# When the layers start beside the sorts, and which rows are asked for ahead of one scatter: two orders changed in a graph kernel

## The chip, the cores and the metric

One core of a Trainium2 chip runs the whole program in one launch. The metric is the device time of that launch in microseconds (us). The engines are named as the profile names them: PE (matrix products), DVE (vector work), ACT (activations and copies), POOL (here: indirect DMAs and one small memset) and SP (plain DMAs). Each engine works through its own queue in order; an instruction that waits holds everything behind it on that engine.

## What is computed

There are 16 graphs of 1024 nodes with 64 channels, an adjacency matrix each, and two residual layers.

```
h = relu(layernorm(x))
# layer 0
adj_d = adjacency with self loops, thinned by a rule on ranks and degrees
s     = values of the live neighbours, sorted per node and channel
agg   = 0.25*quantile(s, 0.25) + 0.5*quantile(s, 0.5) + 0.25*quantile(s, 0.75)
x     = x + mask * (relu((h + agg) @ W1 + b1) @ W2 + b2)        # 64 -> 128 -> 64
# layer 1
h  = relu(layernorm(x))
x1 = bn(relu(adj @ (h  @ W1) + b1))
x2 = bn(relu(adj @ (x1 @ W2) + b2))
x3 = bn(relu(adj @ (x2 @ W3) + b3))
x  = x + relu(concat(x1, x2, x3) @ Wl + bl)
```

## The kernel before

The 16 graphs are treated as 8 pairs. A loop over the pairs thins the adjacency, orders the nodes by degree, and computes the quantiles by sorting networks on DVE (`quantiles`, line L1186 is its compare). The nodes of a pair fall into groups by degree:

- Blocks whose neighbours' rows PE gathers by matrix products (`sort_block`; `sort_pairs` for the few nodes of highest degree, which two or four pairs share; the last of these, the *tails* of pairs 4 to 7, are the 16 nodes of highest degree in each graph).
- Groups of nodes whose neighbours' rows POOL fetches by indirect DMA (`fetch_nodes`, `sort_nodes`). A group has 17, 19 or 21 slots. For each slot POOL issues two *asks* (L1486), numbered a=0 and a=1, and then a memset of a tiny row (L1498), which only keeps the pace. The ask a=0 of a slot waits for the compare that DVE's program had reached when the slot was asked for; the ask a=1 has no such wait and is ordered only behind the memset of the slot before.

The results of a group are written to a buffer in memory, `agg_d`, by indirect scatters on POOL (L1368). The tails' eight scatters (two for each pair, tile `o_tails`) come from `store_tails`.

Behind the loop over pairs stands the last part. There the sorts of pair 7 and the shared groups are still to be done, and beside them runs the generator `later`, which does all of layer 1 and the MLP of layer 0 for pair after pair:

- `load(p)` issues loads on SP (L1693 `xt`, L1694 `h`, L1695 `agg`, L1702 `mk`). The load of `agg` waits for all scatters of that pair.
- `first(p)` is `first_layer`: L1594 adds `h` to `agg`, L1583 transposes, L1603 and L1607 are the MLP's products, L1608, L1610 and L1611 finish layer 0, L624 to L632 are the layernorm, and L1583 transposes its result (`pt`).
- `second(p)` loads the adjacency (`adjT`, L1715) and runs `next_layer`: for each of three layers L1636 `pw` and its three parts (L1637, L1640, L1641, L1642), then 96 products `pg` (L1652) in two halves with L1656 and L1657 behind each; then `pf` (L1668), L1672, L1675 and the output (L1677). Each `pw`, each half of `pg`, and the end is a step of its own.

`weave(sort, (steps, count, first, end), ...)` writes the order by hand: while the parts of one sort are issued, it takes `count` steps of another generator, spread over the given stretch of the sort. `steps(n)` takes `LATE_SHARES[n]` steps of `later`, and `asking(group, first, end, share)` takes a share of a group's slots. What is left at the end of the sorts is run by `ahead.rest()`. Nothing of this is an instruction's final place: a scheduler places the issued instructions on each engine by their order and the stated dependences, and scatters are issued under high priority.

The last part handles the groups in this order: the tails (`steps(5)`), `then[0]` (group 1 of pair 6, 19 slots, `steps(6)`), the shared block of pair 7 (`steps(7)`), `then[1]` (the group that pairs 6 and 7 share, 21 slots, `steps(8)`), `then[2]` (pair 7, 17 slots, `steps(9)`) and `then[3]` (pair 7, 19 slots, `steps(10)`). So the asks of `then[1]` are 42, of `then[2]` 34, of `then[3]` 38.

The lines that put the tails' scatters ahead of later asks are these:

```
                    if sent_ahead[0] is not None:
                        follow(asked, sent_ahead[0])
                        sent_ahead[0] = None
```

`sent_ahead` is set behind the tails' `send`, and the first ask that is issued after it follows the last of these scatters.

Of the kernel before, what the change touches and what calls it, by code (L numbers as in the profile page):

```python
# [56 lines left out]
TAILS = {4: (0, 4), 7: (4, 8)}  # L57
TAIL = (1008, 1024, 21, 42)

MID = len(BLOCKS) - 1  # L60
# [349 lines left out]
def graph_layers_kernel(ctx: ExitStack, tc: tile.TileContext, ins, out: bass.AP):  # L410
    nc = tc.nc
    x_d, adj_d, mask_d = ins["x"], ins["adj"], ins["nodemask"]
    NB, N, _ = x_d.shape
# [3 lines left out]
    NP = NB // 2  # L417
# [62 lines left out]
    for i in range(2 * len(NODES) - 1):  # L480
        _, _, least, slots = NODES[i % 2 if i < 4 else 2]
# [136 lines left out]
    def rows_of(ap):  # L618
        return ap.rearrange("(t p) c -> p t c", p=P)
# [837 lines left out]
    def sort_pairs(n, first, end, g, pools):  # L1457

        work, ps, rows = pools
        block = (BLOCKS + (TAIL,))[n]  # L1460
        W = block[1] - block[0]
        whole = (end - first) * W
        t = rows.tile([P, plan(block)[3], whole], F32, tag="t", bufs=1, name="t_pairs")
        agg = work.tile([P, whole], F32, tag="agg_pairs", name="agg_pairs")
        z = part_z[n] if n == MID else part_z[n][:, :, first:end]
        yield from quantiles(work, block, (g, t), z.rearrange("p q p2 w -> p q (p2 w)"), agg)
        if n > MID:
            store_tails(first, end, agg, pools)
            return
        for p in range(first, end):  # L1470
            waiting.append((p, agg, slice((p - first) * W, (p - first + 1) * W), block[0]))
# [54 lines left out]
    def asking(fetched, first, end, share=1.0):  # L1526

        return fetched[4], math.ceil(share * NODES[fetched[1]][3]), first, end

    def sort_nodes(fetched, pools):  # L1530

        work, ps, rows = pools
        pairs, i, g, z, ask = fetched
        ask.rest()
        j0, j1, _, slots = block = NODES[i]
        W = g.shape[2]
        t = rows.tile([P, plan(block)[3], W], F32, tag="t", bufs=1, name="t_nodes")
        agg = work.tile([P, W], F32, tag="agg_nodes", bufs=1, name="agg_nodes")
        yield from quantiles(work, block, (g, t), z, agg, W // C)
        waiting_nodes.append((pairs, i, agg))  # L1540
# [17 lines left out]
    def weave(sort, *others):  # L1558


        share, taken = 0.0, [0] * len(others)

        def due(share):
            for i, (steps, count, first, end) in enumerate(others):
                while taken[i] < count and first + (end - first) * taken[i] / count <= share:
                    steps.step()
                    taken[i] += 1

        due(0.0)
        for part in sort:  # L1570
            share += part
            due(share)
        due(1.0)
# [106 lines left out]
    def later(pools, keep, done):  # L1680

        one, ps = pools


        def load(p):
            assert p < done.sent
            xt = one.tile([P, NT, 2, C], F32, tag="xt", bufs=2, name="xt")
            h = one.tile([P, NT, 2, C], F32, tag="h", name="h_late")
            agg = one.tile([P, NT, 2, C], F32, tag="agg", name="agg")
            mk = one.tile([P, NT, 2], U8, tag="mk", name="mk")  # L1690
            for x in range(2):
                b = 2 * p + x
                nc.sync.dma_start(out=xt[:, :, x, :], in_=rows_of(x_d[b]))  # L1693
                nc.sync.dma_start(out=h[:, :, x, :], in_=rows_of(h_d[b][:, :]))  # L1694
                load = nc.sync.dma_start(out=agg[:, :, x, :], in_=rows_of(agg_d[p][x * N : (x + 1) * N, :]))  # L1695
                for sent in agg_sent[p]:
                    tc.add_manual_dep(
                        load.ins, sent.ins.name,
                        mybir.DependencyInfo(mybir.DependencyClass.Sync, mybir.DependencyReason.DATA),
                        reason="aggregates of all nodes",  # L1700
                    )
                nc.sync.dma_start(out=mk[:, :, x], in_=mask_d[b])  # L1702
            return xt, h, agg, mk

        def first(xt, h, agg, mk):
            mask = one.tile([P, NT, 2], F32, tag="mask", name="mask")
            nc.vector.tensor_copy(mask, mk)
            cur = yield from first_layer(pools, xt, h, agg, mask)
            return xt, cur

        def second(p, x2, cur):
            adjT = []
            for x in range(2):
                adjT.append(one.tile([P, NT, N], F8, tag=f"adjT{x}", name=f"adjT{x}"))
                nc.sync.dma_start(out=adjT[x], in_=adjT_d[2 * p + x][:, :, :])  # L1715
            yield
            yield from next_layer(pools, [out[2 * p], out[2 * p + 1]], adjT, x2, cur)

        loaded = load(0)
        yield  # L1720
        given = yield from first(*loaded)
        for p in range(NP):
            now = Steps(second(p, *given))
            now.step()
            yield
            ahead = None
            if p + 1 < NP:
                loaded = load(p + 1)
                for _ in range(5):
                    now.step()  # L1730
                    yield
                ahead = Steps(first(*loaded))
            while now.step():
                yield
                if ahead is not None and ahead.step():
                    yield
            if ahead is not None:
                ahead.rest()
                given = ahead.result
# [146 lines left out]
    with ExitStack() as stack:  # L1886
        keep = stack.enter_context(tc.tile_pool(name="keep", bufs=1))
        pools = (
            stack.enter_context(tc.tile_pool(name="work", bufs=1)),
            stack.enter_context(tc.tile_pool(name="ps", bufs=1, space=PSUM)),  # L1890
            stack.enter_context(tc.tile_pool(name="rows", bufs=1)),
        )
        with ExitStack() as inner:
# [19 lines left out]
            for p in range(NP - 1):  # L1913
# [3 lines left out]
                def steps(n):  # L1917
                    return ahead, SHARES[n], 0.0, 1.0
# [6 lines left out]
                both = rows_of_pairs(MID, p, p + 1, p, pools, "g1")  # L1925
# [4 lines left out]
                if p in TAILS:  # L1930
                    tails = rows_of_pairs(MID + 1, *TAILS[p], TAILS[p][1], pools, "g0")
# [13 lines left out]
        with ExitStack() as inner:  # L1945
            one = inner.enter_context(tc.tile_pool(name="late", bufs=1))
            late = (one, inner.enter_context(tc.tile_pool(name="ps_late", bufs=2, space=PSUM)))
            done = Pair()
            done.sent = 4
            ahead = Steps(later(late, keep, done))  # L1950
            def steps(n):
                return ahead, LATE_SHARES[n], 0.0, 1.0

            st = sts[-1]
            weave(sort_block(st, 0, pools), gather_block(st, 1, pools), asking(nodes, 0.0, 0.9), steps(0))
            weave(sort_nodes(nodes, pools), gather_block(st, 2, pools), steps(1))
            nodes = fetch_next()
            then = [fetch_next("r0")]
            weave(sort_block(st, 1, pools), asking(nodes, 0.0, 0.9), steps(2))
            send_nodes()  # L1960
            both = rows_of_pairs(MID, NP - 1, NP, NP - 1, pools, "g1")
            weave(
                sort_block(st, 2, pools), gather_block(st, MID, pools, into=both), asking(then[0], 0.0, 0.9), steps(3)
            )
            tails = rows_of_pairs(MID + 1, *TAILS[NP - 1], NP - 1, pools, "g0")
            weave(sort_nodes(nodes, pools), gather_block(st, MID + 1, pools, into=tails[:, :, -TW:]), steps(4))
            then += [fetch_next(), fetch_next("s"), fetch_next("s")]
            weave(
                sort_pairs(MID + 1, *TAILS[NP - 1], tails, pools), asking(then[1], 0.0, 0.9), steps(5),
            )  # L1970
            send(pools)
            sent_ahead[0] = last_sent[0]
            done.sent = NP - 2
            weave(sort_nodes(then[0], pools), asking(then[2], 0.1, 1.0, 0.6), steps(6))
            send_nodes()
            weave(sort_pairs(MID, NP - 1, NP, both, pools), asking(then[2], 0.0, 0.8), asking(then[3], 0.8, 1.0, 0.1), steps(7))
            send(pools)
            weave(sort_nodes(then[1], pools), asking(then[3], 0.0, 1.0, 0.5), steps(8))
            send_nodes()
            done.sent = NP - 1  # L1980
            weave(sort_nodes(then[2], pools), asking(then[3], 0.0, 0.9), steps(9))
            send_nodes()
            weave(sort_nodes(then[3], pools), steps(10))
            send(pools)
            done.sent = NP
            ahead.rest()
# [49 lines left out]
```

## Time and profile before

| what | value |
|---|---|
| median of 7 runs | 2841.92 us (2833.01 to 2853.05) |
| the profiled execution | 2821.8 us, its span 2819.9 us |
| granted PE clock over the span | 0.864 |
| DVE busy | 2347.3 us (83%) |
| PE busy | 2161.1 us (77%) |
| POOL busy | 1712.0 us (61%) |
| ACT busy | 1618.8 us (57%) |

Times inside the execution are counted from the span's start. The profiled execution is 20 us shorter than the median of the runs. Of the span, the last part with `later` takes the stretch from about 2160 us to the end; the sorts end at 2712.75 us, and 107.15 us follow in which only `later` runs. "Idle before" in a row is how long the engine stood still just before the instruction, with what ended that.

### The profile page before, as it was taken

Reading aid. Unit: us, or ns where it says so; the run is one execution under the profiler, and the core shown is the slowest. Engines: PE = TensorE matmul, PEld = TensorE weight load, DVE = VectorE, ACT = ScalarE, POOL = GpSimd, SP = SyncE. Lnnn points to the kernel's source line nnn. Section 1 sums busy time; section 2 is a strip of 40 time slices with the busy share of each in tenths; the row PEclk is TensorE's granted clock in tenths of the full one; section 3 lists DMA queues with packets and bytes.
Section 4 is the critical chain, followed back from the end, with each engine's and each line's share of the span. In section 5 each row is a group of like instructions: output and inputs, shape, how many; then the busy total and the mean of one; then the engine's idle time right before and its main releaser. Section 6 shows DMA issues by size and latency. Waiting matters only on the chain. (4 is left out here: it accounts for less than half of the span.)

```text
span 2819.9 us, 54826 instructions
## 1 busy us (share of the span) xinstructions
PE 2161.1 (77%) x21220; PEld 1382.0 (49%) x21220; DVE 2347.3 (83%) x5452; ACT 1618.8 (57%) x3255; POOL 1712.0 (61%) x1570
## 2 busy tenths in 40 slices
PE   4668977796789679868974588579858899738888
PEld 3435554454455446535642455355526565425555
DVE  6358998788889889998979999889986988939863
ACT  4564877476758667785867367767673324213222
POOL 7225766485928663774576748674865387988200
PEclk9869988897799789969986799789869988879899
DMA  5114222222322132224252133142213136213221
GB/s 158 57 42 134 59 74 70 86 72 62 76 83 88 48 90 74 83 68 119 63 79 57 28 93 89 47 112 75 74 41 72 24 78 93 67 24 77 68 61 47
DMA packets 262766, 205.43 MB, mean 73 GB/s; under 512 B 218721, under 2 KB 219105, under 8 KB 258401
## 3 DMA queue, kind: packets, MB, share of 16 engines
q1 hardware_dynamic: 178528, 133.61, 16.3%
q0 software_dynamic: 40960, 62.37, 9.2%
q10 hardware_dynamic: 43008, 5.87, 1.8%
q8 instruction: 168, 2.75, 0.4%
q14 instruction: 102, 0.83, 0.1%
HBM read 148.89 MB, written 52.81 MB: 72 GB/s over the span
## 5 line engine op out<-in xcount | busy, mean ns | idle before, releaser
L1486 POOL DMA_INDIRECT g_nodes<-rows_d,rows_listed x744 | 978.3, 1315 | 716.4 <-DVE prod L1198 267.0
L1270 PE MATMUL pg<-s,hp 128*64 128x496 fp8e4 (+5 forms) x8064 | 756.3, 339 | 149.0 <-ACT hp L764 53.0
L1270 PEld LDWEIGHTS <-hp 128*64 128x64 bf16 x8064 | 458.1, 114 | 390.7 <-ACT hp L764 73.9
L1498 POOL MEMSET rest_row<- 1x768 bf16 x372 | 289.2, 777 | 0.1
L1652 PE MATMUL pg<-adjT,xw 128*64 128x512 fp8e4 x2304 | 280.4, 392 | 5.9 <-ACT xw L1641 2.9
L1245 DVE TENSOR_SCALAR s<-r 128x3200 uint16<-128x3200 uint16 (+2 forms) x192 | 206.7, 1085 | 65.1 <-PE pg L1270 48.1
L983 POOL DMA_INDIRECT live_d<-edge,place x128 | 151.7, 1185 | 113.7 <-issue 55.7
L1274 ACT ACTIVATE g<-pg 128x400 f32<-128x400 f32 (+3 forms) x168 | 83.9, 499 | 223.2 <-PE pg L1270 154.2
L1652 PEld LDWEIGHTS <-xw 128*64 128x64 bf16 x2304 | 133.2, 113 | 137.2 <-issue 25.8
L850 ACT ACTIVATE edge<-a 128x1024 fp8e4<-128x1024 uint32 x128 | 135.3, 1058 | 97.6 <-DMA a<-in_adj 95.1
L942 ACT ACTIVATE edge<-q,bias 128x1024 fp8e4<-128x1024 f32 x128 | 142.0, 1110 | 56.9 <-PE q L937 51.0
L1186 DVE TENSOR_TENSOR t<-g 128x800 f32<-128x800 f32 (+9 forms) x184 | 168.3, 928 | 2.8 <-ACT g L1274 0.8
L915 ACT ACTIVATE stays<-cs,back 128x1024 f16<-128x1024 f32 x128 | 138.4, 1113 | 48.9 <-PE cs L911 35.5
L1341 PE MATMUL pg<-s,hp 128*64 128x384 bf16 (+14 forms) x1872 | 152.6, 303 | 16.5 <-DVE s L1310 11.5
L1186 DVE TENSOR_TENSOR t_nodes<-g_nodes 128x256 f32<-128x256 f32 (+6 forms) x192 | 125.4, 663 | 47.7 <-DMA g_nodes<-rows_d,rows_listed 33.7
L1018 PE MATMUL pt<-ident_h,lp 128*128 128x128 bf16 x1024 | 106.8, 274 | 72.6 <-ACT liveT L1024 32.9
L1186 DVE TENSOR_TENSOR g<-t 128x992 f32<-128x992 f32 (+7 forms) x176 | 160.2, 935 | 2.3
L969 ACT ACTIVATE stays<-keys,minus 128x1024 fp8e4<-128x1024 f32 x120 | 134.2, 1119 | 45.8 <-PE keys L954 32.5
L1368 POOL DMA_INDIRECT agg_d<-o,node_of x96 | 136.2, 1418 | 33.8 <-issue 24.9
L857 PE MATMUL ptE<-ident_h,one 128*128 128x128 bf16 x1024 | 84.2, 233 | 77.0 <-DVE one L854 60.9
L1656 ACT ACTIVATE xT<-pg,c_L_gnn_b 128x512 f32<-128x512 f32 x48 | 32.9, 685 | 186.8 <-PE pg L1652 163.1
L1310 DVE TENSOR_SCALAR s<-r 128x192 bf16<-128x192 bf16 (+11 forms) x544 | 115.2, 307 | 29.4 <-remote 15.2
(272 smaller groups left out, 5218.5 us busy)
## 6 DMA issues: line engine op xcount, KB each, us to landing
a<-in_adj SPq DMA_DIRECT2D x128, 512.0 KB
lp<-live_d POOLq DMA_DIRECT2D x32, 514.0 KB
adjT_d<-edgeT SPq DMA_DIRECT2D x16, 1024.0 KB
adjT<-adjT_d SPq DMA_DIRECT2D x16, 1024.0 KB
g_nodes<-rows_d,rows_listed POOLq DMA_INDIRECT x744
room<-in_x SPq DMA_DIRECT2D x16, 256.0 KB
h_again<-h_d SPq DMA_DIRECT2D x16, 256.0 KB
xt<-in_x SPq DMA_DIRECT2D x16, 256.0 KB
```

What stands on the lines that cost most here:

```text
L850: nc.scalar.activation(edge[:, t, :N], a[:, :].bitcast(U32), AF.Sign, accum_out=found[:, 0, b, t : t + 1], saturate=False)
L915: nc.scalar.activation(stays[:, t, :], cs, AF.Abs, bias=back[:, t : t + 1], scale=2.0)
L942: nc.scalar.activation(edge[:, t, :N], q, AF.Relu, bias=bias(-2.0), accum_out=nv[:, t : t + 1], saturate=False)
L983: sent = nc.gpsimd.indirect_dma_start(out=live_d[b][:, :], out_offset=bass.IndirectOffsetOnAxis(ap=place[:, t : t + 1], axis=0), in_=edge[ ...
L1186: sorted_by[0] = nc.vector.tensor_tensor(view(bufs, o, n1, n2), view(bufs, a, n1, n2), view(bufs, b, n1, n2), ALU.max if op else ALU.min)
L1245: nc.vector.tensor_scalar(s[:, j, :, us, :], st.r[0][:, :, us, j0:j1], abs(k - 3), 0x0808, ALU.logical_shift_right if k > 3 else ALU.logic ...
L1270: summed = nc.tensor.matmul(out=pg[x * C : (x + 1) * C, those, :], lhsT=st.hp[:, part, x, u, :], rhs=picked, start=(i == 0 and part == 0), ...
L1341: summed = nc.tensor.matmul(out=pg[x * C : (x + 1) * C, ks, w0:], lhsT=st.hp[:, part, x, u, :], rhs=s[:, ks, x, u, w0:], start=(whole and ...
L1368: sent = nc.gpsimd.indirect_dma_start(out=agg_d[p][:, :], out_offset=bass.IndirectOffsetOnAxis(ap=rows, axis=0), in_=data, in_offset=None)
L1486: asked = nc.gpsimd.indirect_dma_start(out=g[:, k, a * C : (a + 1) * C], out_offset=None, in_=rows_d[st.p][:, :], in_offset=bass.IndirectO ...
L1498: rested[0] = nc.gpsimd.memset(rest_row, 0.0)
L1652: nc.tensor.matmul(out=pg[cs, :], lhsT=part[:, u, cs], rhs=adjT[x][:, u, sl], start=(u == 0 and k == 0), stop=(u == NT - 1 and k == len(xw ...
```

## The change

Two things are changed in the order that is written by hand; no arithmetic, tile or buffer changes.

In `later`, `first(p+1)` starts after two further steps of `second(p)` and not after five. So it alternates with the second half of the first layer's products, the second layer's `pw` and the second layer's products, where it alternated before with the second half of layer 2 and with layer 3.

In the last part, rows are asked for later: of `then[1]` a share of 0.3 beside the tails' sort, and the rest beside the sort of `then[0]`; of `then[2]` and `then[3]` correspondingly later.

```diff
@@ later
                 loaded = load(p + 1)
-                for _ in range(5):
+                for _ in range(2):
                     now.step()
                     yield
                 ahead = Steps(first(*loaded))
@@ last part
             weave(
-                sort_pairs(MID + 1, *TAILS[NP - 1], tails, pools), asking(then[1], 0.0, 0.9), steps(5),
+                sort_pairs(MID + 1, *TAILS[NP - 1], tails, pools), asking(then[1], 0.0, 0.9, 0.3), steps(5),
             )
             send(pools)
             sent_ahead[0] = last_sent[0]
             done.sent = NP - 2
-            weave(sort_nodes(then[0], pools), asking(then[2], 0.1, 1.0, 0.6), steps(6))
+            weave(sort_nodes(then[0], pools), asking(then[1], 0.1, 1.0), steps(6))
             send_nodes()
-            weave(sort_pairs(MID, NP - 1, NP, both, pools), asking(then[2], 0.0, 0.8), asking(then[3], 0.8, 1.0, 0.1), steps(7))
+            weave(sort_pairs(MID, NP - 1, NP, both, pools), asking(then[2], 0.0, 1.0, 0.6), steps(7))
             send(pools)
-            weave(sort_nodes(then[1], pools), asking(then[3], 0.0, 1.0, 0.5), steps(8))
+            weave(sort_nodes(then[1], pools), asking(then[2], 0.0, 0.5), asking(then[3], 0.5, 1.0, 0.3), steps(8))
             send_nodes()
             done.sent = NP - 1
             weave(sort_nodes(then[2], pools), asking(then[3], 0.0, 0.9), steps(9))
```

## Prediction

> **What bounds the kernel now.** I read the page's 40 slices first, to see where DVE, the busiest engine, is not full near the code that changes.
>
> ```profile
> PE   4668977796789679868974588579858899738888
> DVE  6358998788889889998979999889986988939863
> POOL 7225766485928663774576748674865387988200
> ```
>
> A slice is 70.5 us. The 36th (2467 to 2538 us) is the dip: DVE and PE at 3, POOL at 8. The last two slices are the tail, in which PE is full and DVE is not. Next, the stretches around the dip (busy us of PE, PEld, DVE, ACT, POOL):
>
> ```profile
> 2467.00:2490.00 23.00, 7.04 (x56) 3.69 (x52) 4.43 (x11) 1.96 (x3) 18.83 (x22) 0.72 0.10 19
> 2490.00:2510.00 20.00, 0.00 (x0) 0.00 (x0) 0.00 (x0) 0.00 (x0) 16.44 (x20) 0.50 0.13 19
> 2608.00:2679.00 71.00, 59.81 (x426) 37.99 (x425) 62.65 (x125) 19.90 (x42) 20.40 (x17) 0.88 0.29 68
> 2679.00:2713.00 34.00, 23.32 (x171) 16.76 (x171) 33.18 (x68) 6.97 (x11) 0.00 (x0) 0.85 0.32 96
> 2713.00:2765.00 52.00, 51.45 (x416) 31.04 (x410) 22.66 (x31) 15.00 (x25) 1.91 (x2) 1.00 0.20 60
> ```
>
> For 20 us only POOL works. Later POOL has room (20.40 of 71, then nothing), DVE bounds up to 2713, PE behind it. The timeline names the stalled instruction, and the chain that ended last says what it waits for:
>
> ```profile
> 2472.11 0.41 DVE L1186 TENSOR_TENSOR t_nodes<-t_nodes 128x256 f32<-128x256 f32 x1
> 2513.70 1.23 DVE L1594 TENSOR_TENSOR agg<-agg,h_late 128x1024 f32<-128x1024 f32 x1 [41.18 <-issue]
> ```
>
> ```profile
> 2507.28 1.81 DMA agg_d<-o_tails,node_of
> 2509.33 2.96 DMA agg<-agg_d
> 2512.29 1.42 issue
> ```
>
> L1594 is the first instruction of pair 4's `first`. It stands in DVE's queue ahead of most of `then[0]`'s sort, waits for the `agg` load, and that waits for pair 4's two tails' scatters. POOL's timeline shows why those are late: `o_tails` was written by 2461.87 (ACT's row), but POOL was at asks.
>
> ```profile
> 2502.37 0.94 POOL L1486 DMA_INDIRECT g_nodes<-rows_d,rows_listed  x1 [0.30 <-issue]
> 2503.61 0.94 POOL L1486 DMA_INDIRECT g_nodes<-rows_d,rows_listed  x1 [0.30 <-issue]
> 2504.86 0.94 POOL L1486 DMA_INDIRECT g_nodes<-rows_d,rows_listed  x1 [0.30 <-issue]
> 2506.11 0.87 POOL L1368 DMA_INDIRECT agg_d<-o_tails,node_of  x1 [0.30 <-issue]
> 2507.28 0.86 POOL L1368 DMA_INDIRECT agg_d<-o_tails,node_of  x1 [0.30 <-issue]
> ```
>
> **Step 1: POOL ahead of the tails' scatters.** From 2383.32 to 2506.11 POOL issued, without a long pause, 60 asks, 38 memsets and 2 other scatters. In the built order of the changed kernel the same start is followed by 45 asks, 38 memsets and 2 scatters. Only a=0 asks move behind the tails (14 of `then[1]`, one of `then[2]`): an a=1 ask is ordered only behind the memset before it, so all 21 of `then[1]` and all 17 of `then[2]` stay in front. An ask takes 0.94 + 0.30 = 1.24 us where DVE is idle; over the whole stretch it is (122.8 - 38 x 0.89 - 2 x 1.4)/60 = 1.44, with a memset at 0.73 + 0.16 and a scatter at the page's mean of 1.4. So 15 fewer are worth 18.6 to 21.6 us. I take 18.6, as what falls away is the end of the queue, where DVE is idle. First scatter: 2506.1 - 18.6 = 2487.5.
>
> **Step 2: the order among the scatters.** Before, pair 4's are the 1st and 2nd of eight; in the built order they are the 1st and 6th. The sixth starts 5.8 us behind the first (the eight start 1.15 us apart). From pair 4's last scatter to L1594 is 2513.70 - 2507.28 = 6.4 us. So L1594 starts at 2487.5 + 5.8 + 6.4 = 2499.7, 14.0 us sooner; 41 us of stall become some 24, since the layers and sort that are issued ahead of L1594 also grow by six DVE instructions (2.7 us).
>
> **Step 3: DVE from L1594 to the last sort's end.** Before, this takes from 2513.70 to 2712.75, 199.0 us. I add up for its 404 instructions the distance from start to start that the same shape has when it runs back to back (0.34 us for 256 columns, 0.60 for 512, 1.14 for 1024): 182.1 us, so 17 us are idle (4.2 of it at one xT, 2.7 at one L1608). The changed order has 394 instructions here, 176.8 us: six run ahead of L1594 (2.7 us, inside the stall), and four now stand behind the sort's end (two L1672 and L1675 of pair 5 and a small one, 2.6 us). The idle time I can't derive: `first` now lies beside layer 2 and not layer 3, so every wait in it moves. Bounds: 5 us if the better spread hides most, 17 as before, more by the rivals below. I take 14, near the row of before. The last sort ends at 2499.7 + 176.8 + 14 = 2690.5, 22.2 us sooner.
>
> POOL must keep up with that. Behind `then[0]`'s sort it has about 35 asks, 19 memsets and 4 scatters to issue before the last row of `then[2]`: 35 x 1.24 + 19 x 0.89 + 4 x 1.17 = 65 us, or 73 with 1.44 an ask. DVE needs 78 us of back-to-back work (the same sums) from there to the first compare of `then[2]`. So the asks fit, with 5 to 13 us to spare; I cost them at nothing. If that cover goes, the shortfall is added to the sort's end.
>
> The Trainium skill (GPSIMD Engine Reference, Key points) says that POOL shares its SBUF interfaces with DVE and contends with DVE instructions that have two SBUF inputs, as every compare has. The trace agrees (1.24 us an ask with DVE idle, 1.44 on average), and the rule speaks against this change: 15 asks leave the time when DVE is idle for the time of its compares. By the rule they cost 15 x 0.2 = 3 us more of POOL, by the fit above still nothing.
>
> **Step 4: the tail.** Before, 107.15 us follow the last sort. Two things lengthen it.
>
> ```profile
> 2706.88 1.97 PE L1583 MATMUL pt<-ident,agg 128*128 128x128 f32 x8 [10.68 <-DVE agg L632]
> 2708.67 3.16 PE L1636 MATMUL pw<-wl,chan 128*128 128x128 f32 x16
> 2711.77 10.79 PE L1652 MATMUL pg<-adjT,xw 128*64 128x512 fp8e4 x96
> ```
>
> Before, pair 6's first layer starts at 2711.77, 1 us ahead of the sort's end. In the built order its `pw` needs a PSUM buffer that pair 5's L1672 frees, and this L1672 now stands behind the sort's last instruction: two L1672 (1.2), `pw`'s second half and its three parts follow (1.0 + about 1.7), so `pg` starts 3.9 us behind the sort's end: 4.9 us later relative to it. Then pair 7's `first` lies in layer 2 of pair 6. PE's work is the same, but the layernorm's last transposes (`pt`) now head PE's queue in front of layer 3 while DVE finishes L1608 to L632 (10.3 us from py's end to L632's); the half of layer 2 that is still queued covers most, and 2 to 4 us stay open. The rest (`pf`, pair 7's own 52.8 us) is unchanged. Together 7 to 9, I take 8: 115.2 us.
>
> **The sum.** 2690.5 + 115.2 = 2805.7 against 2819.9: -14.2 us. In the pairs 0 to 3 of `later` (2160 to 2472 us) only `range(2)` acts, and there POOL's asks set the pace (a wait of 60 us in POOL's queue ends at 2226, and then POOL is busy to 2365); back-to-back work to L1594 is 274.4 us against 272.0, the six instructions of step 2: cost nothing. The profiled execution becomes 2807.6; it was 0.7% below the median, so the same difference makes 2841.9 - 14.2 = 2828 of the median.
>
> **Rivals.**
> *The asks come back as a wait on rows* (no change, 0.18). Behind the tails POOL's row at 2515.94 shows an ask of 1.91 us plus 0.30 while DVE sorts. If all 35 took 2.2: 77 + 17 + 5 = 99 us against 78 plus some 5 of idle, so `then[2]` waits 16 us, and the sum is about +2. For it: that row. Against it: the mean of 1.44.
> *PE's queue* (slower, 0.28). The transposes that wait for L632 stand in front of layer 3's products for pairs 5, 6 and 7, not in front of the next pair's.
>
> ```profile
> PE pt L1583 <- DVE agg L632: 36.3, 6, 12.3
> ```
>
> Today these waits are 6 us each, 12.3 at most. If each of three pairs pays 6 more, on PE and so on DVE's next xT, the 14.2 are gone by +4; at the full 12.3 it is 23 slower. It decides from 22.7/3 = 7.6 us a pair. Against it: DVE has its sort to do meanwhile, except for pair 7, where I have charged it.
> *The idle time of step 3 shrinks to 5* (0.09): -23 us, 2819.
>
> **How the numbers follow.** About 0.3% (8.5 us) is what a measurement of this kernel can tell from no change. The forecast has 0.45, its own range 2815 to 2832 (idle 5 to 17, 1.24 to 1.44, tail 7 to 9). Faster: 0.43 of it, 0.09, and 0.02 of the rows' case, 0.54. Same: 0.02, 0.10 of the rows' case, 0.05 of PE's queue, 0.17. Slower: 0.06 and 0.23, 0.29. The range reaches from 2814 to 2852: it leaves out the worst of PE's queue above and a gain beyond 28 below.
>
> **What would show it.** Right: the idle before pair 4's L1594 falls from 41.2 to about 24; its scatters are the 1st and 6th; POOL is busy through 2550 to 2620; the last sort ends near 2690 and 115 us follow, with `pg` of pair 6 behind the sort's end. Wrong: a wait of DVE's sort for `g_nodes` of `then[2]` or `then[3]`; PE waiting over 8 us for L632 in pairs 5 or 6; a tail over 120 us; or L1594 later than 2505.

## The result and the profile after

The changed kernel takes 2847.24 us (median of 26 runs) against 2840.09 us of the kernel before: ratio 1.0034, with a 95% interval of 1.0017 to 1.0051. It is slower by about 10 us where 14 us less were forecast. On another chip the same pair gave 1.0008 (0.9986 to 1.0029). The time lies inside the forecast range; the sign is wrong.

The profiled execution is 2847.6 us with a span of 2845.8 us. First its slices:

```profile
PE   4668977796788579769964697589768996748888
DVE  6368998798889889898979998888977996949962
POOL 7334856486828664773677748666774597958400
```

The dip of DVE in the 36th slice (2490 to 2561 us) is still there, 4 where 3 stood, and the 34th (2348 to 2419 us) has fallen from 8 to 6: idle time was spread, not removed. The timeline of DVE names two large waits where there was one:

```profile
2386.74 0.58 DVE L1657 TENSOR_SCALAR xT<-xT,bn_s,c_L_gnn_be 128x512 f32<-128x512 f32 x1 [23.73 <-issue]
2518.26 1.23 DVE L1594 TENSOR_TENSOR agg<-agg,h_late 128x1024 f32<-128x1024 f32 x1 [24.13 <-issue]
```

The row of L1594 is the stall that the change was priced on: 41.18 us before, 24.13 now, and some 24 were forecast. The row of L1657 is new. ACT's timeline shows where it comes from:

```profile
2354.82 1.07 ACT L1586 COPY chan<-pt 128x512 f32<-128x512 f32 x2 [0.25 <-issue]
2385.85 0.27 ACT L1389 COPY o<-pt_agg 128x128 f32<-128x128 f32 x1 [29.96 <-DMA agg_d<-o,node_of]
2386.01 1.27 ACT L1656 ACTIVATE xT<-pg,c_L_gnn_b 128x512 f32<-128x512 f32 x2
```

L1389 copies a block's aggregates into the tile `o`, of which there are three; this copy waits for the scatter of the copy three before it, and that scatter is in POOL's queue behind asks. L1656 stands behind it on ACT, and L1657 on DVE waits for L1656. Before, ACT reached the same copy later, when the scatter was done.

POOL at the tails' scatters, and PE at the start of pair 6 (the same places before are shown in the prediction):

```profile
2506.09 0.87 POOL L1368 DMA_INDIRECT agg_d<-o_tails,node_of  x1 [0.30 <-issue]
```

```profile
2710.81 1.97 PE L1583 MATMUL pt<-ident,agg 128*128 128x128 f32 x8 [11.45 <-DVE agg L632]
2730.37 2.11 PE L1636 MATMUL pw<-wl,chan 128*128 128x128 f32 x16
2732.41 3.35 PE L1652 MATMUL pg<-adjT,xw 128*64 128x512 fp8e4 x26
```

The first tails' scatter is at 2506.09, as late as before, although POOL needs less time for what is ahead of it: 107.3 us from the first ask of `then[1]`, against 122.8. That ask starts 16 us later, and 7 of these were behind already in the loop over the pairs. To leave them out, times are counted below from a common start where it is named: the last L1207 of the shared block that is sorted ahead of the last part. On this count the ask starts at 276.1 us, 9 us later than before (267.2). The new wait on ACT is not the cause: without it the ask starts no sooner (279.4 with a fourth buffer for `o`, 278.8 in a second execution of the order of before), so the profiled execution of before was early here. The last sort ends at 2728.2, and pair 6's first `pg` starts 4.2 us behind it.

Three rows of the chain that ended last matter for the reading of both profiles. Before:

```profile
2603.36 8.92 another core or an unknown queue
```

After:

```profile
2523.41 11.34 another core or an unknown queue
2651.95 8.74 another core or an unknown queue
```

In each of them ACT stands still for some 9 to 11 us, and the trace names nothing that holds it. Such a halt is put down to "remote" in the list of waits, here of ACT, first before and then after:

```profile
ACT g_pairs L1346 <- remote: 29.0, 7, 7.9
```

```profile
ACT g_pairs L1346 <- remote: 36.2, 6, 12.6
```

They do not belong to an order of the kernel. Of the sixteen traces of this case four have 31 to 41 such waits each, in which ACT alone stands for 81 to 116 us; the other twelve have none. The four are before, after and the two runs on the place and the tail apart, taken where the kernel before takes 2840 and 2853 us in the median; beside the twelve it takes 2767 to 2786 us.

The table sets the stretches of the forecast beside each other, for these two executions and for a second one of each order without such halts (of before: the run with a fourth buffer, in which DVE, ACT and POOL have the same instructions in the same order; the second ones are from two chips).

| stretch, us | before | before, again | forecast | after | after, again |
|---|---|---|---|---|---|
| first ask of `then[1]` to first tails' scatter | 122.8 | 124.9 | 104.2 | 107.3 | 108.4 |
| idle before pair 4's L1594 | 41.2 | 53.6 | 24 | 24.1 | 23.5 |
| L1594 to the last sort's end | 199.0 | 190.8 | 190.8 | 209.9 | 193.3 |
| last sort's end to the end | 107.2 | 106.9 | 115.2 | 117.6 | 115.5 |

### The profile page after: what moved, and what is told of

Its sections match the earlier page's. It is cut to its first block, busy times and chain, and to the rows that moved or that the text cites. A ratio compares the mean times of both kernels' runs of the same rounds, so it can differ in the third digit from the quotient of the medians.

```text
span 2845.8 us, 54808 instructions
## 1 busy us (share of the span) xinstructions
PE 2155.7 (76%) x21220; PEld 1380.9 (49%) x21220; DVE 2344.3 (82%) x5452; ACT 1619.9 (57%) x3255; POOL 1744.3 (61%) x1570
## 4 chain that ended last, share of the span: by engine, by line
DVE 32%; PE 22%; ACT 8%; issue 4%; DMA 3%; another core or an unknown queue 2%; POOL 1%; SPq 0%; DVEq 0%; ACTq 0%; POOLq 0%
PE pg L1270 6%; PE pg L1652 5%; DVE t L1186 4%; DVE t_nodes L1186 4%; DVE g_nodes L1186 3%; DVE g L1186 3%; DVE s L1245 3%; DVE g_pairs L1186 2%; DVE t_pairs L1186 2%; ACT stays L969 2%; DVE s L1310 2%; ACT liveT L1024 1%; PE pg L1341 1%; PE py L1607 1%
## 5 line engine op out<-in xcount | busy, mean ns | idle before, releaser
L1486 POOL DMA_INDIRECT g_nodes<-rows_d,rows_listed x744 | 1007.2, 1354 | 726.7 <-DVE prod L1198 271.7
L983 POOL DMA_INDIRECT live_d<-edge,place x128 | 164.7, 1287 | 99.5 <-issue 50.6
L1652 PEld LDWEIGHTS <-xw 128*64 128x64 bf16 x2304 | 139.0, 114 | 131.3 <-issue 24.4
L1186 DVE TENSOR_TENSOR t_nodes<-g_nodes 128x256 f32<-128x256 f32 (+6 forms) x192 | 125.3, 664 | 53.6 <-DMA g_nodes<-rows_d,rows_listed 52.7
L1368 POOL DMA_INDIRECT agg_d<-o,node_of x96 | 127.4, 1327 | 30.0 <-issue 25.0
L1656 ACT ACTIVATE xT<-pg,c_L_gnn_b 128x512 f32<-128x512 f32 x48 | 32.9, 687 | 193.8 <-PE pg L1652 183.7
L1018 PEld LDWEIGHTS <-lp 128*128 128x128 fp8e4 x1024 | 91.3, 125 | 100.5 <-issue 86.5
```

Of the source, the lines that this page charges most:

```text
L983: sent = nc.gpsimd.indirect_dma_start(out=live_d[b][:, :], out_offset=bass.IndirectOffsetOnAxis(ap=place[:, t : t + 1], axis=0), in_=edge[ ...
L1018: nc.tensor.matmul(out=pt[:, u, :], lhsT=lp[:, u * P : (u + 1) * P], rhs=ident_h, start=True, stop=True)
L1186: sorted_by[0] = nc.vector.tensor_tensor(view(bufs, o, n1, n2), view(bufs, a, n1, n2), view(bufs, b, n1, n2), ALU.max if op else ALU.min)
L1486: asked = nc.gpsimd.indirect_dma_start(out=g[:, k, a * C : (a + 1) * C], out_offset=None, in_=rows_d[st.p][:, :], in_offset=bass.IndirectO ...
L1652: nc.tensor.matmul(out=pg[cs, :], lhsT=part[:, u, cs], rhs=adjT[x][:, u, sl], start=(u == 0 and k == 0), stop=(u == NT - 1 and k == len(xw ...
```

## The experiments

All ratios are to the kernel before, run beside them on the same chip; the runs were made on several chips, so that only ratios and stretches are compared from one chip to another.

**The wait for a fourth buffer.** Two kernels differ from after and before in this:

```diff
-        o = work.tile([P, P], F32, tag="o", bufs=3, name="o")
+        o = work.tile([P, P], F32, tag="o", bufs=4, name="o")
-    rest_row = const.tile([1, 768], BF16, name="rest_row")
+    rest_row = const.tile([1, 768], U8, name="rest_row")
```

(the same for `o_tails`; the second edit makes room for the buffer, and the memset then writes a whole 0). For the changed kernel:

> The changed kernel with a fourth buffer for the tile o (the paced memset row made one byte an element to find the room; no other edit, instructions in the same order). Theory A (ACT's copy into o waits for a scatter behind POOL's asks, and that holds xT, DVE and PE): the idle of 23.7 us before L1657 at 2387 goes, the tails' sort ends 10 to 20 us sooner than in the changed kernel, and the time is 8 to 18 us below the changed kernel, so 0 to 8 us below the kernel before. Theory B (POOL's asks are the pace in that stretch, the copy only happens to stand there): the wait moves to another instruction, the time is within 3 us of the changed kernel. Theory C (PE's queue and the tail decide): the stretch to the tails' sort gets shorter but the end gains under 3 us.

For the kernel before:

> Control: the kernel before with the same fourth buffer for o and the same memset row. All theories: no wait at o is there to take away, so within 3 us of the kernel before. If the one byte memset alone changes POOL's pace, it shows here.

Measured: the changed kernel with the buffer 0.9980 (0.9958 to 1.0003), the kernel before with it 0.9992 (0.9974 to 1.0010). The row on DVE in the changed kernel with the buffer:

```profile
2454.79 1.23 DVE L1594 TENSOR_TENSOR agg<-agg,h_late 128x1024 f32<-128x1024 f32 x1 [43.09 <-DMA agg<-agg_d]
```

The wait at L1657 is gone, and DVE reaches the end of the tails' sort 29 us sooner than in the second execution of the changed kernel (333.5 against 363.0 us from the common start). But L1594 starts only 10 us sooner (390.4 against 400.2), as its stall grows from 23.5 to 43.1: POOL sets it. POOL's first ask of `then[1]` starts at the same time in both (279.4 and 279.7); what is shorter is the stretch from there to the tails' scatters (98.7 against 108.4 us), in which more asks run while DVE stands still. So theory A was right on the place. Its price isn't settled by this run: 0.9980 is 8 to 15 us below the changed kernel's 1.0008 and 1.0034, which A forecast, but these ratios are from other chips and their intervals are nearly as wide. The control shows that neither the buffer nor the memset of one byte an element changes the kernel before.

**The two halves of the change.**

```diff
 asks alone:    for _ in range(5), and the new asking(...) lines
 layers alone:  for _ in range(2), and the old asking(...) lines
```

> The asks of the change with the layers as before (five steps). Theory A: the copies into o stand where they stood before, no wait there; pair 4's L1594 starts 14 us sooner and the tail is as before, so 10 to 18 us below the kernel before. Theory B: asks pushed behind come back as waits, within 4 us of before. Theory C: as A, since the tail is unchanged, 10 to 18 us below.

> The layers of the change (two steps) with the asks as before. Theory A: the wait at the copy into o is there (20 to 25 us idle before an L1657 near 2387), the stall at pair 4's L1594 stays at about 40 us, the tail is 8 to 11 us longer: 15 to 25 us above the kernel before. Theory B: only the tail, 5 to 10 us above. Theory C: 8 to 11 us above.

Measured: the asks alone 0.9931 (0.9904 to 0.9958), the layers alone 1.0072 (1.0043 to 1.0101). The stall with the asks alone, and the two waits with the layers alone:

```profile
2476.68 1.23 DVE L1594 TENSOR_TENSOR agg<-agg,h_late 128x1024 f32<-128x1024 f32 x1 [19.90 <-issue]
```

```profile
2324.44 0.59 DVE L1657 TENSOR_SCALAR xT<-xT,bn_s,c_L_gnn_be 128x512 f32<-128x512 f32 x1 [24.84 <-ACT xT L1656]
2473.74 1.23 DVE L1594 TENSOR_TENSOR agg<-agg,h_late 128x1024 f32<-128x1024 f32 x1 [43.66 <-DMA agg<-agg_d]
```

This splits the change into a gain of some 19 us and a loss of some 20. What was called one change is two of opposite sign. With the asks alone L1594 stands 22 instructions further back in DVE's queue than in the change, and 28 further than before: 22 compares of the sort and 6 instructions of the layers more run ahead of the stall, and from L1594 to the last sort's end it takes 176.9 us.

**The layers alone with the fourth buffer** (the two edits above together).

> The layers at two steps with the asks as before and the fourth buffer for o. Theory A (the copy into o holds ACT): the idle of 24.8 us before an L1657 goes. With the stall at pair 4's L1594 set by POOL, that stall takes up what is saved there (43 to 60 us instead of 43.7), so of the 18 us over the kernel before some 5 to 15 are saved. Rival (POOL alone sets the time of L1594 whatever ACT does): under 3 us are saved.

Measured: 1.0068 (1.0048 to 1.0088), about as without the buffer. The row:

```profile
2468.05 1.22 DVE L1594 TENSOR_TENSOR agg<-agg,h_late 128x1024 f32<-128x1024 f32 x1 [62.36 <-DMA agg<-agg_d]
```

Most of what ACT's wait gave back, the stall took: 43.7 became 62.4, and L1594 starts 7 us sooner from the common start (409.2 against 415.9), which the ratios do not show. This speaks for the rival of theory A, POOL; the intervals leave room for the lower end of what A forecast.

**Pair 7's first at five steps**, the fourth buffer kept:

```diff
-                for _ in range(2):
+                for _ in range(5 if p + 2 == NP else 2):
```

> The changed kernel with the fourth buffer for o, and pair 7's first at five steps as before (the pairs before it at two). Tail theory (10 us of the change are lost behind the last sort, since pair 7's first lies in pair 6's layer 2 and pair 6's start waits for pair 5's L1672): the part of it that belongs to pair 7 comes back: the stretch from the last sort's end to the end falls from 109.6 to 99 to 105 us, and the time is 5 to 10 us below the run with only the fourth buffer. Rival (the tail is lost where pair 6's pw stands behind pair 5's L1672, set by the pairs before): under 3 us come back.

Measured: 1.0001 (0.9981 to 1.0021) against 0.9980 without this edit. The tail is 4 us shorter (105.5 against 109.6 us from the start of the last sort's last instruction to the start of the last L1675), but the run is not 5 to 10 us below the one without this edit: it is inconclusive for so small a part.

**Which pairs carry the loss.** The changed kernel was run again, beside two that split the loop:

```diff
-                for _ in range(2):
+                for _ in range(2 if p < 3 else 5):      # pairs 1 to 3 early
+                for _ in range(5 if p < 3 else 2):      # pairs 4 to 7 early
```

> The changed kernel once more, beside the next three on the same chip. All theories: 0.2 to 0.5% above the kernel before. If the 11.4 us in which ACT stood still at pair 4's L1604 (released by nothing that the trace names) belong to the kernel, they are in this trace at the same place; if they fall anywhere, they are not.

> The asks of the change; first(p+1) two steps in for p = 0 to 2, five from p = 3 on. The copies into o stand as in the changed kernel, pair 4's L1594 and the tail as with the asks alone. If the copy's wait is the larger loss of the change: 15 to 20 us above the run with the asks alone, so at the kernel before or just below it. If the place of pair 4's L1594 and the tail are the larger: 4 to 10 us above the asks alone, so 9 to 15 us below the kernel before.

> The asks of the change; first(p+1) five steps in for p = 0 to 2, two from p = 3 on. The copies into o as before, pair 4's L1594 22 instructions earlier on DVE than with the asks alone, the tail of the change. If place and tail are the larger loss: 15 us of sort less beside the stall and 10 us of tail, so 20 to 27 us above the asks alone, 0 to 8 us above the kernel before. If the copy's wait is the larger: 10 us above the asks alone, 9 us below the kernel before.

Measured: the changed kernel 1.0008 (0.9986 to 1.0029), pairs 1 to 3 early 0.9941 (0.9919 to 0.9963), pairs 4 to 7 early 1.0006 (0.9984 to 1.0029). With pairs 1 to 3 early the wait behind the copy into `o` is there in full, and DVE stalls as with the asks alone:

```profile
2348.11 0.59 DVE L1657 TENSOR_SCALAR xT<-xT,bn_s,c_L_gnn_be 128x512 f32<-128x512 f32 x1 [24.86 <-ACT xT L1656]
2482.65 1.23 DVE L1594 TENSOR_TENSOR agg<-agg,h_late 128x1024 f32<-128x1024 f32 x1 [19.53 <-DMA agg<-agg_d]
```

From the common start L1594 comes at 398.5 us, with the asks alone at 400.5. So the most striking new row of the profile, 24 us of idle DVE, costs little or nothing. Theory A falls as the explanation; the loss lies in pairs 4 to 7. With these early the stall is longer:

```profile
2469.63 1.23 DVE L1594 TENSOR_TENSOR agg<-agg,h_late 128x1024 f32<-128x1024 f32 x1 [32.92 <-issue]
```

The two runs are from one chip and have no halts, and there pairs 4 to 7 early take 18 us more in the median than pairs 1 to 3 early. In the traces L1594 comes 2.5 us sooner, from there to the last sort's end it takes 192.6 us and not 177.9, and the tail is 114.3 us and not 107.2. So 12 us go with the place of L1594, behind which the 22 instructions now stand, and 7 with the tail. In the second execution of the changed kernel ACT's halt of 11.3 us at pair 4's L1604 is not there, nor any other, so it is no property of this order.

**The place and the tail apart.**

```diff
-                for _ in range(2):
+                for _ in range(2 if p == 3 else 5):     # pair 4 alone: the place of L1594
+                for _ in range(2 if p > 3 else 5):      # pairs 5 to 7: the tail
```

> The asks of the change; first(p+1) two steps in for p = 3 alone, five for all other pairs. On DVE pair 4's L1594 stands at instruction 4820 as in the change (4842 with the asks alone); the last sort is followed by L1642 as in the kernel before, not by pair 5's L1672. If the place of L1594 costs by itself: the stretch from L1594 to the last sort's end is 190 to 194 us (177 with the asks alone), the tail 99 to 101 us, the time 8 to 14 us above the asks alone, 5 to 11 us below the kernel before. If it costs nothing: as the asks alone, 17 to 20 us below the kernel before.

> The asks of the change; first(p+1) two steps in for p = 4 to 6, five for p = 0 to 3. On DVE pair 4's L1594 stands at 4842 as with the asks alone; the last sort is followed by two L1672 and L1675 of pair 5, as in the change. If the tail costs by itself: the stretch from the last sort's end to the end is 107 to 110 us, the one from L1594 to the last sort's end 176 to 179 us, the time 6 to 10 us above the asks alone, 9 to 13 us below the kernel before. If it is covered: as the asks alone, 17 to 20 us below.

Measured: pair 4 alone 0.9967 (0.9937 to 0.9997), pairs 5 to 7 0.9961 (0.9928 to 0.9993). The rows, first of pair 4 alone, then of pairs 5 to 7:

```profile
2547.36 1.22 DVE L1594 TENSOR_TENSOR agg<-agg,h_late 128x1024 f32<-128x1024 f32 x1 [27.07 <-issue]
```

```profile
2737.21 0.29 DVE L1207 TENSOR_TENSOR agg_nodes<-prod 128x128 f32<-128x128 f32 x1
2737.42 0.68 DVE L1672 TENSOR_TENSOR res<-pf,r_L_gnn_bl 128x512 f32<-128x512 f32 x1
2739.08 0.69 DVE L1672 TENSOR_TENSOR res<-pf,r_L_gnn_bl 128x512 f32<-128x512 f32 x1 [0.98 <-PE pf L1668]
```

Each seems to give back about half of the asks' gain: 0.36 and 0.30 of 0.69 per cent, together 0.66 where pairs 4 to 7 early give back 0.75. But the intervals are as wide as these differences, so that neither half is shown by its own time. With pair 4 alone, the stretch from L1594 to the last sort's end is 201.9 us and the tail 107.7; with pairs 5 to 7 they are 193.7 and 115.9. The expectations of the tail hold only where it is counted as with pair 7's first above, from the start of the last sort's last instruction to the start of the last L1675: 100.0 and 108.4 us. Both first stretches are longer than expected (190 to 194 and 176 to 179). Both traces have halts here, 4.8 us on ACT in the former and 8.5 us at an L1608 in the latter, so they do not settle what the place costs by itself.

**What stays in front of the scatters.** Three kernels, all with five steps, let both asks of a slot wait for the sort behind the tails' `send`, which puts them behind the scatters in fact (`held_all` starts as `[False]`):

```diff
-                    if a == 0 and sorted_by[0] is not None:
+                    if (a == 0 or held_all[0]) and sorted_by[0] is not None:
...
             sent_ahead[0] = last_sent[0]
+            held_all[0] = True
```

With the asks of the change:

> The asks of the change with the layers as before, and behind the tails' send both asks of a slot (not only a=0) wait for the sort's compare. POOL then has 15 asks and 7 memsets ahead of the tails' scatters instead of 46 and 38, and pair 4's are the 1st and 2nd of eight. Theory D (the asks a=1 that stay in front are the rest of the stall): the stall at pair 4's L1594 falls from 20 us to under 12. But POOL then idles some 50 us before the tails and has about 190 us of asks behind them, against some 150 us of DVE to then[3]'s sort: rows of then[2] or then[3] come 15 to 30 us late. Sum: within 15 us of the run with the asks alone, more likely above it. If POOL has more slack than that, 8 to 12 us below it.

With the asks of before:

> The kernel before with one edit: behind the tails' send both asks of a slot wait for the sort's compare. All 42 asks of then[1] still stand ahead of the tails' scatters (43 asks, 21 memsets instead of 60 and 38), those of then[2] behind; the order on DVE is that of before. Theory D: the tails' scatters go out at about 2465 (on the clock of the profile before), the stall of 41 us falls to under 10, rows of then[2] and then[3] are in time (about 140 us of POOL against 170 of DVE), and the time is 25 to 38 us below the kernel before. Rival (the stall only moves to rows or to the layers): 0 to 15 us below.

And with a share of 0.8 of `then[1]` ahead:

> The run in which both asks of a slot wait behind the tails' send, with then[1] at a share of 0.8 ahead of the tails and not 0.3: 35 asks and 17 memsets ahead of the scatters. The stall at pair 4's L1594 stays near the floor set by o_tails (10 us), then[2] and then[3] come less late than with 0.3 (25 us of waits on rows there). 15 to 28 us below the kernel before, at or just below the run of the kernel before with both asks held. If rows are late again, 5 us above that.

Measured: 1.0011 (0.9991 to 1.0030) with the asks of the change, 0.9939 (0.9916 to 0.9962) with those of before, 0.9959 (0.9939 to 0.9979) with 0.8. The rows of the first two:

```profile
2605.00 0.43 DVE L1186 TENSOR_TENSOR t_nodes<-g_nodes 128x256 f32<-128x256 f32 x1 [16.13 <-DMA g_nodes<-rows_d,rows_listed]
```

```profile
2433.93 1.23 DVE L1594 TENSOR_TENSOR agg<-agg,h_late 128x1024 f32<-128x1024 f32 x1 [10.67 <-issue]
```

Held back fully, the asks take the stall at pair 4's L1594 to 2.4 us but come back as a wait on rows (here of `then[3]`'s sort; 19.2 us with the share of 0.8), since POOL idles 44 us ahead of the tails. That is 22 us above the asks alone by the two ratios, where at most 15 were expected. The share of 0.8 gains 11 us; 15 to 28 were expected, or 5 less with late rows, as here. With all of `then[1]` in front and the rest held, the stall falls to 10.7 us. That is the size expected, but the time falls by 17 us where 25 to 38 were expected: the stretch from L1594 to the last sort's end is 202.2 us and not 190.8, for the same instructions; 10 us more of it are gaps, the longest a wait of 4.2 us on rows. This kernel and the one with the asks alone both beat the two kernels of the case; their intervals do not tell them apart.

## Why the prediction was wrong, point by point

**Step 1** (18.6 us off POOL's queue) was near: 122.8 and 124.9 us became 107.3 and 108.4, so 15.5 to 16.5. The missing 2 to 3 us have the size of what the sentence on the Trainium skill (GPSIMD Engine Reference, Key points) set aside, that asks moved from idle DVE time into its compares cost 15 x 0.2 = 3 us more. The traces show the price of an ask, 0.95 us in the mean during the stall and 1.48 to 1.58 beside DVE's work, but not that this is where the 2 to 3 us went: ahead of the scatters 40 asks ran beside DVE's work before and 39 after (20 and 6 in the stall), and what rose is the mean of the former, from 1.48 to 1.58. In the second executions they are 32 and 39, at 1.57 in both.

**Step 2** held in the stall: 24.1 us for 24, pair 4's scatters 1st and 6th. L1594 was to come 14 us sooner. From the common start it comes 11 us sooner in the second executions (400.2 against 411.3 us) and 2 in the profiled ones (395.6 against 397.5); the two of the order of before differ by 14 between themselves.

**Step 3** is the step that failed. It forecast 8 us less from L1594 to the last sort's end (199.0 to 190.8); executions without halts give 2.5 us more (190.8 to 193.3). The end value was nearly right; the start value was not. Of the idle time in the stretch before, which the step took for the kernel's own (17 us by its sums; 14.7 counted as gaps between instructions), 8 us belonged to one halt of ACT (the row at 2603.36). The two waits that the step names, 4.2 us at an xT and 2.7 at an L1608, stand right behind it, the first in this row:

```profile
2612.98 0.55 DVE L1657 TENSOR_SCALAR xT<-xT,bn_s,c_L_gnn_be 128x512 f32<-128x512 f32 x1 [4.21 <-ACT xT L1656]
```

In the second execution of that order the gaps are 6.8 us; in the second one of the changed order they are 13.8, and in the five other traces without halts in which pair 4's `first` starts two steps in, they are 13.0 to 14.4. So earlier layers add 7 us of waits there, and the step forecast a saving of 3. The largest are at an L1642 behind the stall, which waited less before, and at pair 5's L1594, which did not wait at all. The L1642 in the second execution of before:

```profile
2479.35 0.69 DVE L1642 TENSOR_TENSOR xw<-rest,xw 128x512 bf16<-128x512 f32 x1 [0.90 <-ACT xw L1641]
```

Both in the second execution of the changed order:

```profile
2483.65 0.69 DVE L1642 TENSOR_TENSOR xw<-rest,xw 128x512 bf16<-128x512 f32 x1 [2.98 <-ACT xw L1641]
2518.96 1.23 DVE L1594 TENSOR_TENSOR agg<-agg,h_late 128x1024 f32<-128x1024 f32 x1 [2.81 <-issue]
```

The fit of POOL's asks that the step costs at nothing held; its upper sum is 72 us and not 73, which changes nothing.

**Step 4** held: 8.6 us more tail (115.5 against 106.9) for 8, and pair 6's `pg` 4.2 us behind the sort's end for 3.9.

**The sum** with what the second executions show: -11 + 2.5 + 8.6 = 0, against -14.2; of the difference 11 us are step 3's and 3 step 2's. That agrees with the 1.0008 of the chip on which the changed order's second execution was taken. The 1.0034 leaves some 10 us that these two traces do not name. It was measured where the halts fall; whether they make the difference or chance does is not shown. The two profiled executions are no fair pair: from the common start they differ by 19 us (703.7 and 723.1), and both have halts in the stretch.

**The flat zero for pairs 0 to 3** missed a wait: a copy into `o` behind a scatter in POOL's queue, 24 us of idle DVE. The price of nothing still nearly held, for the reason given there: POOL's asks set the pace up to pair 4's L1594.

**The rivals.** Rows did not come late in the change; they did when more asks were held back. PE's waits for L632 did not grow in sum:

```profile
PE pt L1583 <- DVE agg L632: 30.4, 7, 11.4
```

That is 30.4 us in seven waits, against 36.3 in six. Slower came true without the mechanism that was named for it. Two of the prediction's signs of being wrong came true: L1594 stands at 2518.26, later than 2505, though counted from the common start it is sooner; and PE waits over 8 us for L632 in pair 6, 11.45, but 10.68 stood there before, so this sign could not tell the orders apart.

**What the prediction did not ask** is what each half does alone. The asks alone move L1594 28 instructions back and free POOL's queue, and gain 19 us together; the layers take 22 of these instructions back and lengthen the tail. Step 2 counted the six against the kernel before and so could not see it.

## What to carry to other kernels

A forecast made against one profiled execution inherits that execution's accidents: look in the chain for halts that nothing released, take them out of the stretch before it is compared, and profile the same order a second time on another chip. An idle row of 24 us can be worth next to nothing while another queue sets the time of the next meeting point; find that point, and ask of every saving ahead of it what is waiting there. Where a change has two edits, price each alone: the place of one blocked instruction in an in-order queue decides how much work hides behind its stall.

## What the runs showed of the hardware

ACT, and more seldom DVE, stood still for up to 12.6 us with no releaser that the trace names (on the shown stretches 8.92 us before; 11.34 and 8.74 after; 8.54 in the run with pairs 5 to 7). In these traces such waits go with where and when a kernel was measured, and not with its order of instructions: 31 to 41 of them in each of four traces, none in twelve others, among these a second execution of both orders. What they are stays open.

An ask takes 0.95 us in the mean on POOL while DVE stands in its stall, and 1.48 to 1.58 us ahead of the tails beside DVE's work, in the four executions of the table; single ones there took up to 9.4 us. With the 0.30 us to the next ask it is the 1.24 us of the prediction, and 15 asks fewer saved 15.5 to 16.5 us.
